# Folding expert biases into the expert weights, and one transpose of denominators for both image halves, in an attention and mixture-of-experts kernel

## Chip, cores and metric

The kernel runs on one core of one Trainium2 chip. The metric is the device time of one execution in microseconds (us); the time before is the median of three runs. One further execution was recorded by the hardware profiler; its span is 1886.6 us.

A core has five engines with queues of their own: PE (TensorE, matrix products and transposes, with weight loads listed as PEld), DVE (VectorE), ACT (ScalarE), POOL (GpSimd) and SP (SyncE, which here only issues transfers). Each works through its instructions in a fixed order and waits for the others by semaphores.

## The reference, cut to what matters

Four images of 32 x 128 x 128 numbers pass through two layers, all in float32.

```python
# layer 0, per image: 4096 tokens of 128 channels
energy = q^T q / (|q_i| |q_j|);  attn = softmax(energy)
x = gamma * (q attn^T) + q
# layer 1, on the same numbers, read as tokens of 128
t = t + linear_attention(ln(t), Wk, Wq, Wv)      # 8 heads
n = ln(t)                                        # mean 0 over the 128 numbers of a row
p = softmax(n @ router_w + router_b); top 2 of 8 experts, renormalised
t = t + sum over the two chosen e of p_e * (n @ expert_w[e] + expert_b[e])
```

The softmax of layer 0 needs one denominator per token; the kernel keeps the denominators as columns (one number per partition) and has to divide a tile in which tokens lie along the row. The expert bias is weighted with the gate `p_e` of its expert.

## The kernel before

A generator `attend` writes the attention of image b. Another generator, `layer1`, writes layer 1 of image b-1; its steps are dealt out between the steps of `attend`, so that both run beside each other. Layer 1 of the last image has nothing to run beside: it forms the tail (`alone`).

The attention step, and the transfers that turn a tile of exponentials for its second use:

```python
pe = ps_e.tile(...); nc.tensor.matmul(pe[:, c0:], qn[jc][:, ts(j, P)], qn[i][:, c0:], ...)   # L276
nc.scalar.activation(pr[:, c0:], pe[:, c0:], AF.Exp, accum_out=sums[:, t, i : i + 1])        # L278
nc.tensor.matmul(po[:, lo:hi], qT[...], w, ...)                                              # L244
nc.vector.transpose(Fb[:, :, :, j, :], pr)                                                   # L285
for a in range(4):
    for q in range(4):
        nc.sync.dma_start(G[ts(q, S), a]..., F[ts(a, S), q]...)                              # L299
# 56 units later: nc.tensor.matmul(pg, qT, G) L213, row sums of G on ACT L218, o += pg on DVE L223
```

The division (one call for each of four quarters of an image; `s` is the half of the channels' rows):

```python
rd = reciprocal(den); rd = rd * gam
def divide(kc):
    df = work.tile([P, 8, HW2, 2], F32, tag="wide", ...)
    for s in range(2):
        ch = 2 * kc + s
        pb = psum_s(...)
        for j in range(NJ):                                   # NJ = 4
            nc.tensor.transpose(pb[:, ts(j, P)], rd[:, blk : blk + 1].to_broadcast([P, P]), ident)   # L383
        for r2 in range(2):
            rows = slice(r2 * 64, r2 * 64 + 64)
            nc.vector.tensor_tensor(df[s*64 : s*64+64, :, :, r2], o[rows]..., pb[rows]..., ALU.mult) # L387
        if s == 1:
            nc.gpsimd.tensor_tensor(tk, tk, df..., ALU.add)   # L395, T += df
        yield
```

Then row statistics, normalisation, the linear attention (`gram`, `pgv`, `pm`, `pat`), row statistics again (rsf, nbf), the router (`route(0)` for rows of groups 0 to 3, `route(1)` for 4 to 7), and the experts:

```python
gate = stat.tile([P, KT + 12, E], ...)
def transpose_gate(g):
    nc.tensor.transpose(pt[:, :P], gate[:, 4 * g : 4 * g + 16, :]..., ident)      # L563
    gates[g] = work.tile([P, P], ..., tag="gT"); nc.vector.tensor_copy(gates[g], pt[:, :P])   # L565
transpose_gate(0)
yield
for g in range(KT // 4):                                      # 8 groups of 4 blocks of 128 rows
    nc.tensor.matmul(pb, gates[g], ebd..., start=True, stop=True)                 # L571, bias of 4 blocks
    nc.vector.tensor_tensor(acc, T[:, ts(g, 4), :], pb..., ALU.add)               # L573
    yield
    for jj in range(2):
        for jk in range(2):
            nc.tensor.matmul(py, xn[:, k, :], ew_sb[:, 0:4, :], ...)              # L581
            for e in range(4): acc[j] = py[e] * gate[k, e] + acc[j]               # DVE, L583
            yield
            nc.tensor.matmul(py, xn[:, k, :], ew_sb[:, 4:8, :], ...)              # L588
            for e in range(4): tmp[jk, e] = py[e] * gate[k, 4 + e]                # ACT, L590
            yield
        # POOL: three adds, L594, L595, L599 (fold tmp, add it to acc)
        if jj == 0 and g + 1 < KT // 4:
            transpose_gate(g + 1)
    # four output transfers from acc, L603
```

Of the kernel before, what the change touches and what calls it, by code (L numbers as in the profile page):

```python
# [10 lines left out]
F32 = mybir.dt.float32  # L11
BF16 = mybir.dt.bfloat16
AF = mybir.ActivationFunctionType
ALU = mybir.AluOpType
# [5 lines left out]
def kernel(  # L20
# [35 lines left out]
    nc = tc.nc  # L56
    P = 128
# [42 lines left out]
    rw_sb = const.tile([P, E], F32, tag="rw", name="rw_sb")  # L100
    rb_sb = const.tile([P, 1, E], F32, tag="rb", name="rb_sb")
    ew_sb = const.tile([P, E, D], F32, tag="ew", name="ew_sb")
    ebd = const.tile([P, 4, D], F32, tag="eb", name="ebd")
    nc.vector.memset(ebd, 0.0)
    at_sb = const.tile([P, NH, D], F32, tag="at", name="at_sb")
    wvx = const.tile([P, NH, D + E], F32, tag="wvx", name="wvx")
    matx = const.tile([P, D + 2 * E], F32, tag="matx", name="matx")
# [5 lines left out]
    def load_weights():  # L113
        nc.scalar.dma_start(gam, gamma.partition_broadcast(P))
        nc.scalar.dma_start(rb_sb[:, 0, :], router_b.partition_broadcast(P))
        nc.scalar.dma_start(rw_sb, router_w)
        for j in range(4):
            nc.scalar.dma_start(ebd[E * j : E * j + E, j, :], expert_b)
        nc.scalar.dma_start(ew_sb, expert_w.rearrange("e d c -> d e c"))

    def setup_weights():
        raw = big1.tile([P, 3, NH, D], F32, tag="xn", name="raw_w")
        wk_sb, wq_sb, wv_sb = raw[:KQ, 0], raw[:KQ, 1], raw[:, 2]
        nc.scalar.dma_start(wk_sb, wk.rearrange("h k d -> k h d"))
        nc.scalar.dma_start(wq_sb, wq.rearrange("h k d -> k h d"))
        nc.scalar.dma_start(wv_sb, wv.rearrange("h e d -> e h d"))
        yield
        for g in range(NH // 4):
            pa = psum_t(f"pa_{g}")
            pv = psum_t(f"pv_{g}")  # L130
            for j in range(4):
                h = 4 * g + j
                nc.tensor.matmul(pa[:, ts(j, D)], wk_sb[:, h, :], wq_sb[:, h, :], start=True, stop=True)
                nc.tensor.transpose(pv[:, ts(j, D)], wv_sb[:, h, :], ident)
            nc.vector.tensor_copy(at_sb[:, 4 * g : 4 * g + 4, :], pa.rearrange("p (h d) -> p h d", d=D))
            nc.vector.tensor_copy(wvx[:, 4 * g : 4 * g + 4, :D], pv.rearrange("p (h d) -> p h d", d=D))
            yield
        pw = psum_t("pw")
        for h in range(NH):
            nc.tensor.matmul(pw[:, ts(h, E)], wv_sb[:, h, :], rw_sb, start=True, stop=True)  # L140
        ones = work.tile([P, P], F32, tag="gT", name="ones")
        nc.vector.memset(ones, 1.0)
        nc.tensor.matmul(pw[:, ts(NH, E)], ones, rw_sb, start=True, stop=True)
        nc.vector.tensor_copy(wvx[:, :, D:], pw[:, : NH * E].rearrange("p (h e) -> p h e", e=E))
        nc.vector.tensor_copy(srw[:, 0, :], pw[:, ts(NH, E)])
        nc.vector.tensor_copy(matx[:, D + E :], rw_sb)
        yield

    def tokens(ap, b):
        return ap[b].rearrange("c (s k r) w -> s r c k w", s=2, r=2)  # L150
# [166 lines left out]
    def layer1(b, st, alone):  # L317
# [24 lines left out]
        nc.vector.tensor_reduce(den, st["sums"], AX.X, ALU.add)  # L342
        rd = stat.tile([P, NB], F32, tag="rd", name=f"rd_{b}")
        nc.vector.reciprocal(rd, den)
        nc.vector.tensor_scalar(rd, rd, gam, None, ALU.mult)
        yield

        rsa, nba, sda = (stat.tile([P, KT, 1], F32, tag=nm, name=f"{nm}_{b}", bufs=1) for nm in ("rsa", "nba", "sda"))
        rsf, nbf = (stat.tile([P, KT, 1], F32, tag=nm, name=f"{nm}_{b}", bufs=1) for nm in ("rsf", "nbf"))

        def row_stats(nm, u, rs_all, nb_all):

# [22 lines left out]

        def divide(kc):
            df = work.tile([P, 8, HW2, 2], F32, tag="wide", name=f"df_{b}_{kc}")
            for s in range(2):
                ch = 2 * kc + s
                pb = psum_s(f"pbd_{b}_{ch}")  # L380
                for j in range(NJ):
                    blk = NJ * ch + j
                    nc.tensor.transpose(pb[:, ts(j, P)], rd[:, blk : blk + 1].to_broadcast([P, P]), ident)  # L383
                o = st["o"][ch]
                for r2 in range(2):
                    rows = slice(r2 * 64, r2 * 64 + 64)
                    nc.vector.tensor_tensor(  # L387
                        df[s * 64 : s * 64 + 64, :, :, r2],
                        o[rows].rearrange("p (k w) -> p k w", w=HW2),
                        pb[rows].rearrange("p (k w) -> p k w", w=HW2),  # L390
                        ALU.mult,
                    )
                if s == 1:
                    tk = T[:, ts(kc, 8), :]
                    nc.gpsimd.tensor_tensor(tk, tk, df.rearrange("p k w r -> p k (w r)"), ALU.add)  # L395
                yield
# [56 lines left out]


        lg = stat.tile([P, KT, E], F32, tag="lg", name=f"lg_{b}", bufs=1)
        gate = stat.tile([P, KT + 12, E], F32, tag="gate", name=f"gate_{b}", bufs=1)
        nc.gpsimd.memset(gate[:, KT:, :], 0.0)
        normed = {}

        def attention_rows(u):  # L460
# [17 lines left out]
        def norm_rows(g):  # L478
            xg = work.tile([P, 4, D], F32, tag="grp", name=f"xg_{b}_{g}", bufs=3)
            for j in range(4):  # L480
                normalise(xg[:, j, :], 4 * g + j, rsf, nbf)
            normed[g] = xg

        def expert_rows(g):
# [48 lines left out]
        for u in range(6):  # L533
            if 0 <= u - 1 < 4:
                la = yield from attention_rows(u - 1)
            for g in (2 * u, 2 * u + 1):
                if u < 4 and not alone:
                    transpose_rows(g)
                    yield
            if 0 <= u - 1 < 4:  # L540
                yield from row_stats(f"f{b}", u - 1, rsf, nbf)
                yield
                router_rows(u - 1, la)
                yield
            for g in (2 * u - 4, 2 * u - 3):
                if 0 <= g - 1:
                    expert_rows(g - 1)
                    yield
                if 0 <= g:
                    norm_rows(g)  # L550
                    yield
            if u in (2, 4):
                yield from route(u // 2 - 1)
# [2 lines left out]


        dst = tokens(out, b)
        gates = {}

        def transpose_gate(g):
            pt = psum_s(f"ptg_{b}_{g}")
            nc.tensor.transpose(pt[:, :P], gate[:, 4 * g : 4 * g + 16, :].rearrange("p j e -> p (j e)"), ident)  # L563
            gates[g] = work.tile([P, P], F32, tag="gT", name=f"gT_{b}_{g}", bufs=2)
            nc.vector.tensor_copy(gates[g], pt[:, :P])  # L565

        transpose_gate(0)
        yield
        for g in range(KT // 4):
            pb = psum_s(f"pbe_{b}_{g}")  # L570
            nc.tensor.matmul(pb, gates[g], ebd.rearrange("p j c -> p (j c)"), start=True, stop=True)  # L571
            acc = work.tile([P, 4, D], F32, tag="acc", name=f"acc_{b}_{g}", bufs=2)
            nc.vector.tensor_tensor(acc, T[:, ts(g, 4), :], pb.rearrange("p (j c) -> p j c", c=D), ALU.add)  # L573
            yield
            for jj in range(2):
                tmp = work.tile([P, 2, 4, D], F32, tag="wide", name=f"tmp_{b}_{g}_{jj}")
                for jk in range(2):
                    j = 2 * jj + jk
                    k = 4 * g + j
                    py = psum_y(f"py_{b}_{k}_0")  # L580
                    nc.tensor.matmul(py, xn[:, k, :], ew_sb[:, 0:4, :], start=True, stop=True)  # L581
                    for e in range(4):
                        nc.vector.scalar_tensor_tensor(  # L583
                            acc[:, j, :], py[:, ts(e, D)], gate[:, k, e : e + 1], acc[:, j, :], ALU.mult, ALU.add
                        )
                    yield
                    py = psum_y(f"py_{b}_{k}_1")
                    nc.tensor.matmul(py, xn[:, k, :], ew_sb[:, 4:8, :], start=True, stop=True)  # L588
                    for e in range(4):
                        nc.scalar.activation(  # L590
                            tmp[:, jk, e, :], py[:, ts(e, D)], AF.Copy, scale=gate[:, k, 4 + e : 5 + e]
                        )
                    yield
                nc.gpsimd.tensor_tensor(tmp[:, :, 0:2], tmp[:, :, 0:2], tmp[:, :, 2:4], ALU.add)  # L594
                nc.gpsimd.tensor_tensor(tmp[:, :, 0], tmp[:, :, 0], tmp[:, :, 1], ALU.add)  # L595
                if jj == 0 and g + 1 < KT // 4:
                    transpose_gate(g + 1)
                rows = acc[:, 2 * jj : 2 * jj + 2, :]
                nc.gpsimd.tensor_tensor(rows, rows, tmp[:, :, 0], ALU.add)  # L599
            for s in range(2):  # L600
# [15 lines left out]
    for b in range(B):  # L616
# [3 lines left out]
        if b == 0:  # L620
            for kc, begin, end in ((1, 0, 5), (2, 6, 20), (3, 25, 45)):
                streams.append((prep(0, kc, states[0]), begin, end, 10))
            streams.append((setup_weights(), 50, 60, 4))
        else:
            streams.append((layer1(b - 1, states[b - 1], False), 7, 97, 161))
        if b + 1 < B:
# [58 lines left out]
```

## Time and profile before

| what | value | where from |
|---|---|---|
| time | 1888.73 us (1886.93 to 1889.08) | median of three runs |
| PE busy | 1799.0 us, 95% of the span | profile, engines |
| DVE, ACT, POOL busy | 909.5, 974.6, 293.7 us | profile, engines |
| mean granted PE clock | 0.983 | profiled run |
| layer 1 of the last image, alone | from about 1732 us to the end | timeline |
| L571, bias product | 64 instructions (2 for each float32 product) | groups |
| L563, transposes of gates | 32 | groups |
| L383, transposes of denominators | 128 | groups |

Busy time is the union of an engine's instructions in the trace. One float32 product of 128x512 appears as two matmul instructions. Matmuls overlap in the records, so that what one costs is read from the distance between starts in the timeline, not from its duration.

### The profile page before, as it was taken

The page shows a single profiled execution, that of the slowest core. Times are in us where ns is not written, and L with a number is a line of the kernel's source. Part 1 is how long each engine was busy: PE and PEld are TensorE (multiplying, and loading weights), DVE is VectorE, ACT ScalarE, POOL GpSimd, SP SyncE. Part 2 cuts the span into 40 slices and gives each one's busy share as a digit, 9 for nine tenths or more (in the row PEclk, how much of TensorE's full clock was granted, in tenths as well). Part 3 has the DMA queues.
Part 4 walks back from the last instruction along what each step waited for, and adds up shares of the span by engine and source line. Part 5 has one row for each costly group of instructions (what it writes and reads, how often), then busy time and mean ns, then how long its engine had stood idle before and what let it go on. Part 6 is the DMA issues. An engine that isn't in the chain of part 4 may idle for free.

```text
span 1886.6 us, 21105 instructions
## 1 busy us (share of the span) xinstructions
PE 1799.0 (95%) x5474; PEld 915.4 (49%) x5474; DVE 909.5 (48%) x2201; ACT 974.6 (52%) x3117; POOL 293.7 (16%) x279
## 2 busy tenths in 40 slices
PE   6999999998999999999999999999899999999678
PEld 4444544454555444455555444445465544444533
DVE  3343224345364454636355455453536445554576
ACT  3454444446457454555556655454554755554455
POOL 0000000002010122212000022220300012221336
PEclk9999999999999999999999999999999999999789
DMA  5333343332233232342233323234233223335001
GB/s 119 80 84 87 78 104 91 89 89 64 61 95 83 65 89 65 86 105 64 64 85 81 92 62 90 68 88 99 53 79 81 72 63 92 81 74 119 1 11 34
DMA packets 142247, 145.68 MB, mean 77 GB/s; under 512 B 32528, under 2 KB 84784, under 8 KB 142128
## 3 DMA queue, kind: packets, MB, share of 16 engines
q1 hardware_dynamic: 138496, 142.73, 31.5%
q10 hardware_dynamic: 3632, 1.60, 0.4%
q8 instruction: 45, 0.74, 0.2%
q14 instruction: 74, 0.61, 0.1%
HBM read 18.38 MB, written 8.39 MB: 14 GB/s over the span
## 4 chain that ended last, share of the span: by engine, by line
PE 81%; DVE 7%; SPq 4%; POOL 3%; ACT 2%; DMA 1%; issue 1%; ACTq 0%; POOLq 0%; DVEq 0%
PE po L244 23%; PE pe L276 20%; PE pg L213 18%; PE py L588 5%; PE py L581 5%; SPq L299 4%; PE pbe L571 1%; PE pat L468 1%; PE pgram L413 1%; DVE F L285 1%; PE ptd L255 1%; POOL rsa L111 1%; DVE df L387 1%; POOL T L395 1%; PE ptn L199 1%
## 5 line engine op out<-in xcount | busy, mean ns | idle before, releaser
L278 ACT ACTIVATE pr<-pe 128x512 f32<-128x512 f32 (+1 forms) x576 | 322.7, 560 | 519.6 <-PE pe L276 513.9
L244 PE MATMUL po<-pr,qT 128*128 128x512 f32 (+3 forms) x1152 | 551.1, 561 | 16.4 <-ACT pr L278 11.6
L285 DVE STREAM_TRANSPOSE F<-pr 128x512 f32<-128x512 f32 x448 | 311.4, 704 | 354.0 <-ACT pr L278 336.5
L276 PE MATMUL pe<-qn,qn 128*128 128x512 f32 x896 | 459.7, 595 | 0.0
L213 PE MATMUL pg<-G,qT 128*128 128x512 f32 x896 | 440.8, 594 | 1.7 <-DVE o L223 1.6
L244 PEld LDWEIGHTS po<-pr,qT 128*128 128x128 f32 x1152 | 213.3, 191 | 249.0 <-issue 182.9
L218 ACT ACTIVATE junk<-G 128x512 bf16<-128x512 f32 x448 | 277.1, 626 | 3.6 <-DMA G<-F 2.8
L213 PEld LDWEIGHTS pg<-G,qT 128*128 128x128 f32 x896 | 167.4, 191 | 196.0 <-issue 186.8
L590 ACT ACTIVATE tmp<-py,gate 128x128 f32<-128x128 f32 x512 | 146.3, 368 | 172.1 <-PE py L588 171.1
L583 DVE SCALAR_TENSOR_TENSOR acc<-py,gate,acc 128x128 f32<-128x128 f32 x512 | 177.7, 349 | 118.3 <-PE py L581 104.6
L276 PEld LDWEIGHTS pe<-qn,qn 128*128 128x128 f32 x896 | 160.9, 191 | 145.3 <-issue 144.4
L223 DVE TENSOR_TENSOR o<-o,pg 128x512 f32<-128x512 f32 x112 | 76.6, 684 | 184.4 <-PE pg L213 183.7
L594 POOL TENSOR_TENSOR tmp<-tmp 128x512 f32<-128x512 f32 x64 | 81.2, 1269 | 534.6 <-ACT tmp L590 534.6
L581 PE MATMUL py<-ew_sb,xn 128*128 128x512 f32 x256 | 132.7, 601 | 1.9 <-ACT tmp L590 1.2
L588 PE MATMUL py<-ew_sb,xn 128*128 128x512 f32 x256 | 131.9, 597 | 2.2 <-DVE acc L583 1.4
L278 ACT ACTIVATION_READ_ACCUMULATOR pr<-pe 128x1 f32 x576 | 114.5, 199 | 0.0
L111 POOL TENSOR_TENSOR rn<-ss,neg_half 128x8 f32<-128x8 f32 x16 | 26.2, 1639 | 500.4 <-DVE ss L185 500.4
L276 PE MATMUL pe<-qn 128*128 128x512 f32 (+3 forms) x256 | 90.3, 444 | 0.0
L218 ACT ACTIVATION_READ_ACCUMULATOR junk<-G 128x1 f32 x448 | 88.5, 198 | 0.0
L370 ACT ACTIVATE xn<-T,nba,rsa 128x128 f32<-128x128 f32 x128 | 51.9, 481 | 55.1 <-DVE nba L367 55.1
L111 POOL TENSOR_TENSOR rsf<-dm_f,neg_half 128x8 f32<-128x8 f32 x16 | 26.3, 1642 | 342.5 <-DVE dm_f L365 342.5
L588 PEld LDWEIGHTS py<-ew_sb,xn 128*128 128x128 f32 x256 | 48.5, 191 | 61.9 <-issue 53.0
(121 smaller groups left out, 1416.5 us busy)
## 6 DMA issues: line engine op xcount, KB each, us to landing
G<-F SPq DMA_DIRECT2D x1792, 64.0 KB, 2.0
xx<-in_x_dram SPq DMA_DIRECT2D x64, 128.0 KB, 2.8
T<-in_x_dram SPq DMA_DIRECT2D x16, 512.0 KB, 7.1
out_dram<-acc SPq DMA_DIRECT2D x128, 64.0 KB, 1.8
ew_sb<-in_L_ffn_expert_w_dram ACTq DMA_DIRECT2D x1, 512.0 KB, 5.4
raw_w<-in_L_attn_Wv_dram ACTq DMA_DIRECT2D x1, 512.0 KB
raw_w<-in_L_attn_Wk_dram ACTq DMA_DIRECT2D x1, 256.0 KB
raw_w<-in_L_attn_Wq_dram ACTq DMA_DIRECT2D x1, 256.0 KB
```

The source lines that it names most:

```text
L213: nc.tensor.matmul(pg.rearrange("p (a f) -> p a f", a=4), st["qT"][i][:, ib, :], G[:, :, ib], start=(ib == 0), stop=(ib == NJ - 1),)
L218: nc.scalar.activation(junk, G[:, :, ib], AF.Copy, accum_out=st["sums"][:, NJ * i + ib, jc : jc + 1])
L223: nc.vector.tensor_tensor(o, o, pg.rearrange("p (a j c) -> p a j c", a=4, c=S), ALU.add)
L244: nc.tensor.matmul(po[:, lo:hi], qT[blk // NJ][:, blk % NJ, :], w, start=(count[0] == 1), stop=(count[0] == total))
L276: nc.tensor.matmul(pe[:, c0:], qn[jc][:, ts(j, P)], qn[i][:, c0:], start=True, stop=True)
L278: nc.scalar.activation(pr[:, c0:], pe[:, c0:], AF.Exp, accum_out=sums[:, t, i : i + 1])
L285: nc.vector.transpose(Fb[:, :, :, j, :], pr)
L581: nc.tensor.matmul(py, xn[:, k, :], ew_sb[:, 0:4, :], start=True, stop=True)
L583: nc.vector.scalar_tensor_tensor(acc[:, j, :], py[:, ts(e, D)], gate[:, k, e : e + 1], acc[:, j, :], ALU.mult, ALU.add)
L588: nc.tensor.matmul(py, xn[:, k, :], ew_sb[:, 4:8, :], start=True, stop=True)
L590: nc.scalar.activation(tmp[:, jk, e, :], py[:, ts(e, D)], AF.Copy, scale=gate[:, k, 4 + e : 5 + e])
L594: nc.gpsimd.tensor_tensor(tmp[:, :, 0:2], tmp[:, :, 0:2], tmp[:, :, 2:4], ALU.add)
```

## The change

It has two parts.

**Expert biases.** A row `n` out of the layer norm has mean 0 over its 128 entries. If `W' = W + (1/128) (b - colsum(W))`, with the same row added to each row of W, then `(n + 1) @ W' = n @ W + b`: the 1 brings in `colsum(W) + b - colsum(W) = b`, and `n` against a constant column gives 0. So the expert weights are changed once, at set-up (two products with a matrix of ones and four DVE operations), the rows are normalised with a bias that is 1 larger (`nbo`), and the bias product, the transposes of gates, their copies and the separate start of `acc` go away.

**Denominators.** Halves s = 0 and 1 are put side by side into one 128x128 tile for each j (64 columns of each), gamma is applied while it is filled, and one transpose serves both. `divide` has three steps then, not two.

```diff
-    ebd = const.tile([P, 4, D], F32, tag="eb", name="ebd")
-    nc.vector.memset(ebd, 0.0)
...
+        eb = work.tile([P, E, D], F32, tag="wide", name="eb")
+        nc.scalar.dma_start(eb, expert_b.partition_broadcast(P))
+        for h in range(2):
+            half = ew_sb[:, 4 * h : 4 * h + 4, :]
+            pc = psum_t(f"pc_{h}")
+            nc.tensor.matmul(pc, ones, half, start=True, stop=True)
+            pe3 = pc.rearrange("p (e d) -> p e d", d=D)
+            dev = eb[:, 4 * h : 4 * h + 4, :]
+            nc.vector.tensor_tensor(dev, dev, pe3, ALU.subtract)
+            nc.vector.scalar_tensor_tensor(half, dev, 1.0 / D, half, ALU.mult, ALU.add)
+            yield
...
-        nc.vector.tensor_scalar(rd, rd, gam, None, ALU.mult)
...
-            for s in range(2):
-                ch = 2 * kc + s
-                pb = psum_s(f"pbd_{b}_{ch}")
-                for j in range(NJ):
-                    blk = NJ * ch + j
-                    nc.tensor.transpose(pb[:, ts(j, P)], rd[:, blk : blk + 1].to_broadcast([P, P]), ident)
+            pb = psum_s(f"pbd_{b}_{kc}")
+            wide = work.tile([P, NJ, 2, 64], F32, tag="grp", name=f"rdx_{b}_{kc}", bufs=3)
+            for s in range(2):
+                one = rd[:, NJ * (2 * kc + s) : NJ * (2 * kc + s + 1), None]
+                nc.vector.tensor_scalar(wide[:, :, s], one.to_broadcast([P, NJ, 64]), gam, None, ALU.mult)
+            yield
+            for j in range(NJ):
+                nc.tensor.transpose(pb[:, ts(j, P)], wide[:, j].rearrange("p s c -> p (s c)"), ident)
...
-                normalise(xg[:, j, :], 4 * g + j, rsf, nbf)
+                normalise(xg[:, j, :], 4 * g + j, rsf, nbo)
...
                 yield from row_stats(f"f{b}", u - 1, rsf, nbf)
+                nc.vector.tensor_scalar(nbo[:, ts(u - 1, 8)], nbf[:, ts(u - 1, 8)], 1.0, None, ALU.add)
...
-        transpose_gate(0)
-        yield
         for g in range(KT // 4):
-            pb = psum_s(f"pbe_{b}_{g}")
-            nc.tensor.matmul(pb, gates[g], ebd.rearrange("p j c -> p (j c)"), start=True, stop=True)
             acc = work.tile([P, 4, D], F32, tag="acc", name=f"acc_{b}_{g}", bufs=2)
-            nc.vector.tensor_tensor(acc, T[:, ts(g, 4), :], pb.rearrange("p (j c) -> p j c", c=D), ALU.add)
-            yield
...
                         nc.vector.scalar_tensor_tensor(
-                            acc[:, j, :], py[:, ts(e, D)], gate[:, k, e : e + 1], acc[:, j, :], ALU.mult, ALU.add
+                            acc[:, j, :], py[:, ts(e, D)], gate[:, k, e : e + 1],
+                            T[:, k, :] if e == 0 else acc[:, j, :], ALU.mult, ALU.add,
                         )
...
-                if jj == 0 and g + 1 < KT // 4:
-                    transpose_gate(g + 1)
...
-            streams.append((setup_weights(), 50, 60, 4))
+            streams.append((setup_weights(), 50, 62, 6))
```

The number of steps after which `layer1` is dealt out (161 between 7% and 97% of an image's attention) is left as it is.

More of the change, by code (lines that the diff above doesn't have):

```diff
@@ L116, in load_weights @@
         nc.scalar.dma_start(rw_sb, router_w)
-        for j in range(4):
-            nc.scalar.dma_start(ebd[E * j : E * j + E, j, :], expert_b)
         nc.scalar.dma_start(ew_sb, expert_w.rearrange("e d c -> d e c"))
@@ L140, in setup_weights @@
             nc.tensor.matmul(pw[:, ts(h, E)], wv_sb[:, h, :], rw_sb, start=True, stop=True)
-        ones = work.tile([P, P], F32, tag="gT", name="ones")
+        ones = work.tile([P, P], F32, tag="sq", name="ones", bufs=1)
         nc.vector.memset(ones, 1.0)
@@ L344, in layer1 @@
         nc.vector.reciprocal(rd, den)
-        nc.vector.tensor_scalar(rd, rd, gam, None, ALU.mult)
         yield
         rsa, nba, sda = (stat.tile([P, KT, 1], F32, tag=nm, name=f"{nm}_{b}", bufs=1) for nm in ("rsa", "nba", "sda"))
-        rsf, nbf = (stat.tile([P, KT, 1], F32, tag=nm, name=f"{nm}_{b}", bufs=1) for nm in ("rsf", "nbf"))
+        rsf, nbf, nbo = (stat.tile([P, KT, 1], F32, tag=nm, name=f"{nm}_{b}", bufs=1) for nm in ("rsf", "nbf", "nbo"))
         def row_stats(nm, u, rs_all, nb_all):
@@ L377, in divide @@
             df = work.tile([P, 8, HW2, 2], F32, tag="wide", name=f"df_{b}_{kc}")
+            pb = psum_s(f"pbd_{b}_{kc}")
+            wide = work.tile([P, NJ, 2, 64], F32, tag="grp", name=f"rdx_{b}_{kc}", bufs=3)
             for s in range(2):
-                ch = 2 * kc + s
-                pb = psum_s(f"pbd_{b}_{ch}")
-                for j in range(NJ):
-                    blk = NJ * ch + j
-                    nc.tensor.transpose(pb[:, ts(j, P)], rd[:, blk : blk + 1].to_broadcast([P, P]), ident)
-                o = st["o"][ch]
+                one = rd[:, NJ * (2 * kc + s) : NJ * (2 * kc + s + 1), None]
[4 more added lines that the diff above has]
+            for s in range(2):
+                own = slice(s * 64, s * 64 + 64)
+                o = st["o"][2 * kc + s]
                 for r2 in range(2):
@@ L387, in divide @@
                     nc.vector.tensor_tensor(
-                        df[s * 64 : s * 64 + 64, :, :, r2],
+                        df[own, :, :, r2],
                         o[rows].rearrange("p (k w) -> p k w", w=HW2),
-                        pb[rows].rearrange("p (k w) -> p k w", w=HW2),
+                        pb[own].rearrange("p (k w) -> p k w", w=HW2),
                         ALU.mult,
@@ L455, in layer1 @@
         lg = stat.tile([P, KT, E], F32, tag="lg", name=f"lg_{b}", bufs=1)
-        gate = stat.tile([P, KT + 12, E], F32, tag="gate", name=f"gate_{b}", bufs=1)
-        nc.gpsimd.memset(gate[:, KT:, :], 0.0)
+        gate = stat.tile([P, KT, E], F32, tag="gate", name=f"gate_{b}", bufs=1)
         normed = {}
@@ L558, in layer1 @@
         dst = tokens(out, b)
[L559 to L565, printed above, removed]
-        transpose_gate(0)
-        yield
         for g in range(KT // 4):
-            pb = psum_s(f"pbe_{b}_{g}")
-            nc.tensor.matmul(pb, gates[g], ebd.rearrange("p j c -> p (j c)"), start=True, stop=True)
             acc = work.tile([P, 4, D], F32, tag="acc", name=f"acc_{b}_{g}", bufs=2)
-            nc.vector.tensor_tensor(acc, T[:, ts(g, 4), :], pb.rearrange("p (j c) -> p j c", c=D), ALU.add)
-            yield
             for jj in range(2):
```

## Prediction

> **What bounds the kernel now.** I began with the page's engine shares and its chain that ended last.
>
> ```profile
> PE 1799.0 (95%) x5474; PEld 915.4 (49%) x5474; DVE 909.5 (48%) x2201; ACT 974.6 (52%) x3117; POOL 293.7 (16%) x279
> PE 81%; DVE 7%; SPq 4%; POOL 3%; ACT 2%; DMA 1%; issue 1%; ACTq 0%; POOLq 0%; DVEq 0%
> ```
>
> PE looks like the bound. To see whether this holds in every stage, I cut the span into windows (columns: stage, its length, then busy us and instructions of PE, PEld, DVE, ACT and POOL, granted PE clock, DMA share, GB/s).
>
> ```profile
> 560.00:700.00 140.00, 139.93 (x394) 67.46 (x393) 70.97 (x165) 80.73 (x254) 19.95 (x20) 1.00 0.32 78
> 700.00:850.00 150.00, 149.48 (x410) 71.34 (x409) 68.66 (x139) 78.11 (x265) 29.26 (x32) 1.00 0.36 87
> 850.00:1000.00 150.00, 143.15 (x506) 79.84 (x506) 80.91 (x218) 78.13 (x242) 22.68 (x13) 0.97 0.30 72
> 1750.00:1800.00 50.00, 35.62 (x210) 30.61 (x211) 30.97 (x136) 25.22 (x61) 14.80 (x9) 0.81 0.00 1
> 1800.00:1886.00 86.00, 68.87 (x166) 30.48 (x164) 63.27 (x214) 45.82 (x150) 47.01 (x50) 0.90 0.11 25
> ```
>
> While experts run beside attention (560 to 850), PE has no gap: 289.4 of 290 us. Around the division (850 to 1000) it idles 7 us per image. Only the tail from 1732 differs: PE idles there and DVE is nearly as busy.
>
> What a removed instruction costs is the distance of starts. The PE timeline (start, length, instruction):
>
> ```profile
> 1644.17 1.02 PE L213 MATMUL pg<-G,qT 128*128 128x512 f32 x2
> 1645.03 1.02 PE L571 MATMUL pbe<-ebd,gT 128*128 128x512 f32 x2
> 1645.89 1.02 PE L276 MATMUL pe<-qn,qn 128*128 128x512 f32 x2
> ...
> 1319.37 0.60 PE L383 MATMUL pbd<-ident,rd 128*128 128x128 f32 x4
> 1319.81 1.02 PE L276 MATMUL pe<-qn,qn 128*128 128x512 f32 x2
> ```
>
> A bias product takes 1645.89 - 1645.03 = 0.86 us of PE, as does every other 128x512 product; four transposes take 0.44 us, 0.11 each.
>
> **What the Trainium skill says.** "Perfetto Trace Analysis", Identifying the Most-Contended Engine: busy share of matmuls is a poor measure of the distance to the roofline, as matmuls are pipelined. The trace agrees: a pair is listed with 1.02 us and costs 0.86; so I count starts. "TensorE: Matmul & The Clock Gate", Part 4: a 128x128 transpose lasts some 275 ns in a kernel, mostly latency. The trace has a median of 273 ns for L383, yet a cost of 110 ns in a row. "VectorE: DVE Perf Modes", The TRN2 errata: a float32 tensor_tensor takes (N+151)/0.96 ns, 691 ns for N = 512; the trace has 687 ns for L573. I use the formula for the new 256-element fills of `wide`: (256+151)/0.96 = 424 ns, an estimate and rather an upper limit. The first-named TensorE page, Part 1: the clock halves after an idle window of some 3.4 us. The tail shows it: 0.52 granted between 1745 and 1760.
>
> **The change, part by part. Beside attention (images 0 to 2).** Removed from PE: 3 x 8 = 24 bias products x 0.86 = 20.6 us; 24 transposes of gates x 0.11 = 2.6 us; of 128 transposes of denominators half go, 16 per image, 48 x 0.11 = 5.3 us. Sum 28.5 us. The first two lie in stretches without a gap on PE, so I count them in full; the third partly falls into waits, but there a quarter now needs one PSUM tile and one turn of PE, not two, which should ease the same waits.
>
> On DVE 24 x (0.687 + 0.284) = 23 us go (L573, L565), and 24 x 0.42 + 12 x 0.17 (`nbo`, as the 8-column L365) = 12 us come. DVE is half idle there: worth nothing.
>
> Set-up: 2 products x 0.86 = 1.7 us on a PE without gaps; four DVE operations of about 0.7 us. The broadcast of 512 KB of biases is issued in the same step in which DVE needs it; the weights of that size landed in 5.4 us. If DVE really waits for it, tiles of exponentials back up, but there are six of them. I charge 1 us. Net beside attention: -28.5 + 2.7 = -25.8 us.
>
> **The tail.** Each group of four blocks is a strict PE sequence:
>
> ```profile
> 1831.23 1.02 PE L571 MATMUL pbe<-ebd,gT 128*128 128x512 f32 x2
> ...
> 1835.52 0.27 PE L563 MATMUL ptg<-ident,gate 128*128 128x128 f32 x1
> ...
> 1839.07 1.02 PE L571 MATMUL pbe<-ebd,gT 128*128 128x512 f32 x2
> ```
>
> The period is 7.84 us: eight expert products (6.87) + bias (0.86) + transpose (0.11). Without the last two it is 6.87, if DVE keeps up: its four accumulations of a block take 1.51 us, 6.04 a group; ACT needs 4 x 1.14 = 4.6, POOL 2 x (1.27 + 0.73 + 0.73) = 5.5. PE stays the bound. Eight groups x 0.97 = 7.8 us.
>
> There is a second gain. Between the first gates and the steady run PE waits:
>
> ```profile
> 1804.43 0.28 DVE L530 TENSOR_TENSOR gate<-oh,dn 128x128 f32<-128x128 f32 x1
> ...
> 1815.79 0.68 DVE L573 TENSOR_TENSOR acc<-T,pbe 128x512 f32<-128x512 f32 x1
> 1816.59 0.34 DVE L583 SCALAR_TENSOR_TENSOR acc<-py,gate,acc 128x128 f32<-128x128 f32 x1
> ...
> 1819.87 0.20 PEld L563 LDWEIGHTS ptg<-ident,gate 128*128 128x128 f32 x2 [0.82 <-DVE gate L530]
> ```
>
> The gates of groups 0 to 3 are there at 1804.7, and two blocks of products lie in PSUM since 1801; but the first accumulation comes at 1816.6, because acc begins with the bias, and its gate transpose stands in PE's queue behind transposes that wait for ACT. Moreover, the transpose for group 1 takes in 16 blocks, hence gates of the second half, which are ready only at 1819.8. After the change accumulation can start at 1804.7. DVE is then busy with statistics and routing, with some 3.7 us idle to 1820; with the 0.97 us of bias work gone it can fit about 13 more accumulations, three blocks, before 1820: 3 x 1.72 = 5 us. That rests on the order in which the build lays DVE's instructions, so I take half: 2.5 us. The division in the tail: the extra fills of quarters 0 and 1 lie under the 10.1 us load of T, and later ones lose their second turn of PE (`pbd` at 1763.1, among other transposes); I take 1 us gain. Tail: 7.8 + 2.5 + 1 = 11.3 us.
>
> **Sum.** 1888.7 - 25.8 - 11.3 = 1851.6; I say **1851 us**, a ratio of 0.980, on the very border of 2%.
>
> **Rivals.** (1) *The SP queue becomes the bound.* Sixteen issues for a tile take 10.0 us, and four bare attention steps take 4 x 3 x 0.86 = 10.3 us of PE: near. For it: the chain runs through these issues from 1710 to 1732, and `layer1`, with some six steps fewer while still dealt out as 161, ends at about 93.5% of an image, leaving a longer bare stretch. Against it: 100 to 200 is bare attention with PE busy 100.00 of 100 us, while SP makes 134 issues, 84 us at the 0.63 between issues in a row. It would give back up to 8 us: 1859. (2) *Waits around the division grow.* ACT's eight normalisations in one run block exponentials (PE waits 5 us at 1347 for ACT). The three-step division moves these runs against the diagonal tiles, where PE has nothing else to do; three images x 3 us either way: 1842 to 1860. (3) *DVE bounds the tail.* Its work from 1804.7 on is 66 us less 7.5; it could end at 1863, against 1879 now. If the build starts accumulation at once, the tail gains 15 us, not 11: 1847. (4) *The removed bias work was hidden anyway*, as PE's records are modelled. Then only the set-up cost would be seen: 1891. Windows without a gap and the exact 0.86 spacing speak against it.
>
> **Range and chances.** The counted PE work (36 us with the tail's groups) is firm; the reordering of waits I put at 8 us either way beside attention (three divisions at about 3 us each) and 5 us in the tail (from no gain beyond the count to DVE's limit). As these need not fall together, I take about 12 us on each side: 1839 to 1864. The border of 2% is 1851.0, so faster by over 2% and within 2% are even: 0.49 and 0.50. A loss of over 2% would need a new 38 us wait: 0.01.
>
> **What would show it right or wrong.** L571, L563, L565 and L573 gone, L383 at 64, PE busy near 1764; the stages with experts still without a PE gap but shorter by 8 to 9 us per image; the tail's group period 6.87 us; the first L583 of the tail soon after the first `gate`. It is wrong if PE gaps open where there were none (then ask what they wait for: G's transfers mean rival 1, ACT rival 2), or if the tail's period stays above 7 us with DVE full.

## The result, and the profile after

The changed kernel takes 1865.45 us (median of 4 runs, 1860.99 to 1865.79) against 1888.9 us before: a ratio of 0.9872, with a 95% interval of 0.9855 to 0.9889. The gain is 23.5 us; 37.1 had been worked out, and the time lies 1.5 us above the range.

The page of the changed kernel, engine shares and the chain that ended last:

```profile
PE 1765.7 (95%) x5318; PEld 890.3 (48%) x5318; DVE 893.4 (48%) x2184; ACT 972.8 (52%) x3117; POOL 293.5 (16%) x275
PE 78%; DVE 12%; POOL 4%; ACT 2%; SPq 2%; DMA 1%; issue 1%; DVEq 0%; POOLq 0%; ACTq 0%
```

PE lost 33.3 us of work, but the span only 22.7: PE's gaps grew from 87.6 to 98.2 us. The chain runs less through PE (78%, not 81%) and more through DVE (12%, not 7%). Stages of the changed kernel (length, then busy us and instructions of PE, PEld, DVE, ACT and POOL, granted PE clock, DMA share, GB/s):

```profile
560.00:700.00 140.00, 139.85 (x414) 69.42 (x413) 67.42 (x175) 83.68 (x265) 18.54 (x18) 1.00 0.33 81
700.00:850.00 150.00, 149.71 (x404) 71.05 (x403) 70.39 (x141) 78.69 (x268) 32.20 (x34) 1.00 0.37 88
850.00:1000.00 150.00, 141.67 (x493) 77.24 (x492) 81.74 (x223) 77.24 (x240) 22.75 (x13) 0.98 0.30 71
```

Beside the experts PE still has no gap (289.56 of 290 us). Around the division it now idles 8.3 us, where it idled 6.9. The timeline of the expert stage and of the tail:

```profile
1622.50 1.02 PE L587 MATMUL py<-ew_sb,xn 128*128 128x512 f32 x2
1623.35 1.02 PE L579 MATMUL py<-ew_sb,xn 128*128 128x512 f32 x2
1624.21 1.02 PE L285 MATMUL pe<-qn,qn 128*128 128x512 f32 x2
...
1794.37 0.28 DVE L541 TENSOR_TENSOR gate<-oh,dn 128x128 f32<-128x128 f32 x1
...
1798.76 0.35 DVE L581 SCALAR_TENSOR_TENSOR acc<-py,gate,T 128x128 f32<-128x128 f32 x1
...
1821.04 1.88 PE L579 MATMUL py<-ew_sb,xn 128*128 128x512 f32 x4
...
1827.90 1.88 PE L579 MATMUL py<-ew_sb,xn 128*128 128x512 f32 x4
```

No bias product stands between the expert products any more; a group of eight in the tail takes 1827.90 - 1821.04 = 6.86 us (7.84 before), and the first accumulation follows the first gates by 4.4 us (12.2 before). The expert half of the change did what was counted. The division did not. What PE waited for (total us, times, longest), first in the kernel before, then in the changed one:

```profile
PE po L244 <- ACT pr L278: 11.6, 11, 1.9
...
PE ptd L255 <- ACT gd L257: 9.0, 3, 5.1
PE pbd L383 <- DVE df L387: 8.9, 3, 7.8
PE pgram L413 <- ACT xn L370: 8.5, 2, 5.4
...
PE pg L213 <- DVE o L223: 1.6, 2, 0.8
```

```profile
PE pgram L425 <- ACT xn L378: 28.8, 6, 19.3
PE po L253 <- ACT pr L287: 17.4, 12, 4.6
...
PE pg L222 <- DVE o L232: 6.3, 6, 1.4
```

The products `po` wait longer for ACT, and `pg` for DVE. The growth of `pgram` is smaller than it looks: 24.8 of its 28.8 us lie in the tail, where the kernel before already waits 17.4 us, in front of `pgram` and of the division's `pbd` together. The 9.0 us of `ptd`, the diagonal tiles' transposes, are gone. To see which stage the loss belongs to, I took six starts from each timeline: the first energy product (`pe`) of images 0 and 1, the last one of image 3, the tail's first `T += df`, its first `gate`, and the end. All in us:

| profile of | to first product | image 0 | images 1 to 3 | to first `T += df` | to first `gate` | to the end | span |
|---|---|---|---|---|---|---|---|
| before | 19.7 | 354.7 | 1355.4 | 15.8 | 58.8 | 82.2 | 1886.6 |
| changed | 21.6 | 358.2 | 1334.0 | 17.4 | 63.2 | 69.6 | 1863.9 |
| changed, again | 19.3 | 358.2 | 1334.0 | 17.3 | 63.2 | 69.5 | 1861.6 |
| bias part alone | 19.2 | 358.2 | 1330.6 | 17.6 | 59.1 | 69.6 | 1854.3 |
| division alone | 19.3 | 354.6 | 1364.9 | 14.7 | 63.0 | 80.8 | 1897.3 |

Both kernels with the new division are the slower ones of their pair in images 1 to 3, and need 4 us more up to the first gate. (The profile of the division alone is of a run of 1899.07 us, 4.1 under the median of its runs.)

### The profile page after: what moved, and what is told of

It is laid out like the page before. It is cut to its first block, busy times and chain, and to the rows that moved or that the text cites. A ratio compares the mean times of both kernels' runs of the same rounds, so it can differ in the third digit from the quotient of the medians.

```text
span 1863.9 us, 20794 instructions
## 1 busy us (share of the span) xinstructions
PE 1765.7 (95%) x5318; PEld 890.3 (48%) x5318; DVE 893.4 (48%) x2184; ACT 972.8 (52%) x3117; POOL 293.5 (16%) x275
## 4 chain that ended last, share of the span: by engine, by line
PE 78%; DVE 12%; POOL 4%; ACT 2%; SPq 2%; DMA 1%; issue 1%; DVEq 0%; POOLq 0%; ACTq 0%
PE po L253 22%; PE pe L285 20%; PE pg L222 18%; PE py L579 5%; PE py L587 5%; DVE df L399 2%; SPq L308 2%; DVE F L294 2%; POOL rsa L109 1%; PE pat L479 1%; PE ptd L264 1%; POOL T L407 1%; ACT xn L378 1%; POOL rn L109 1%; POOL rsf L109 1%
## 5 line engine op out<-in xcount | busy, mean ns | idle before, releaser
L253 PE MATMUL po<-pr,qT 128*128 128x512 f32 (+3 forms) x1152 | 552.7, 562 | 21.3 <-ACT pr L287 17.4
L581 DVE SCALAR_TENSOR_TENSOR acc<-py,gate,acc 128x128 f32<-128x128 f32 x384 | 132.7, 349 | 11.5
L587 PE MATMUL py<-ew_sb,xn 128*128 128x512 f32 x256 | 130.2, 600 | 1.2 <-ACT tmp L589 1.2
L579 PE MATMUL py<-ew_sb,xn 128*128 128x512 f32 x256 | 129.2, 594 | 2.1 <-DVE acc L581 2.0
L581 DVE SCALAR_TENSOR_TENSOR acc<-py,gate,T 128x128 f32<-128x128 f32 x128 | 44.7, 349 | 114.5 <-PE py L579 109.8
## 6 DMA issues: line engine op xcount, KB each, us to landing
eb<-in_L_ffn_expert_b_dram ACTq DMA_DIRECT2D x1, 512.0 KB, 10.3
```

Of the source, the lines that this page charges most:

```text
L253: nc.tensor.matmul(po[:, lo:hi], qT[blk // NJ][:, blk % NJ, :], w, start=(count[0] == 1), stop=(count[0] == total))
L581: nc.vector.scalar_tensor_tensor(acc[:, j, :], py[:, ts(e, D)], gate[:, k, e : e + 1], T[:, k, :] if e == 0 else acc[:, j, :], ALU.mult, A ...
```

## The experiments

**The two parts apart.** First the bias part with the old division, then the new division with the old biases.

```diff
 # e1_bias_only: changed kernel, divide() of before
+        nc.vector.tensor_scalar(rd, rd, gam, None, ALU.mult)
-            wide = work.tile([P, NJ, 2, 64], ...)   # fills, yield, 4 transposes
+            for s in range(2): ... 4 transposes of rd columns each, two steps
 # e2_div_only: kernel before, divide() of the change
```

> The bias part alone; the division is the old one (gamma in rd, two PSUM tiles and eight transposes a quarter). Theory A, the new division costs more than it saves: beside attention 24 bias products and gate transposes fewer, 23.2 us, less 2.8 us of set-up; 2.7 us lost before the first product, as in the changed kernel; from the first gate to the end of the tail 12.7 us less, as in the changed kernel; tail up to the first gate as in the kernel before. Sum 30 us less than before: 1859 us, 6 us faster than the full change. Rival B, the division brought its 6 us and the bias part is short of its sum: 1871 us, slower than the full change.

Measured: 1855.99 us (1851.29 to 1856.12), ratio 0.9819 [0.9805, 0.9832]: -32.7 us.

> The new division alone, biases as before. Theory A: tail 4 us longer up to the first gate (two fills held for 2.3 us each while GpSimd adds to T), one fill held for 1.9 us in each image beside attention and PE gaps around it; 5 us of PE work less. 1889 to 1894 us, no faster than before. Rival B: 64 transposes fewer and one PSUM turn a quarter: 1883 us.

Measured: 1903.18 us (1898.86 to 1903.67), ratio 1.0069 [1.0056, 1.0081]: +14.5 us. So the bias part brings more than the whole change, and the division, meant to save, costs. The two do not add: -32.7 + 14.5 = -18.2, where the change as a whole gives -23.5 (-26.2 when repeated, below). The division costs more beside the old biases than on top of the bias part; why was not taken apart. The waits of PE with the division alone:

```profile
PE pgram L416 <- ACT xn L369: 27.6, 4, 18.3
PE po L244 <- ACT pr L278: 14.3, 11, 4.6
...
PE pg L213 <- DVE o L223: 6.0, 6, 1.3
```

These three are close to those of the changed kernel, without any of its bias part. What follows looks for the reason in the division.

**Was the first profile typical?** The changed kernel unaltered, and once more with the four small bias loads kept ahead of the expert weights in ACT's queue, as the kernel before has them.

```diff
 # e3_keep_loads
+    ebd = const.tile([P, 4, D], F32, tag="eb", name="ebd"); nc.vector.memset(ebd, 0.0)
+        for j in range(4):
+            nc.scalar.dma_start(ebd[E * j : E * j + E, j, :], expert_b)
 # e5_after_again: no edit
```

> The full change, but the four small loads of the expert biases stay in ScalarE's queue ahead of the expert weights, into a tile that nothing reads. Theory A, the start is later because the weights' loads (2.5 MB with the broadcast biases) are now issued 2.8 us sooner and share the transfers with the first image rows: first product of qn at 19.7 us again instead of 21.6, time 1863 us, 2 to 2.7 us less than the full change. Rival B, the late start is chance or comes from elsewhere: 1865.5 us and 21.6 us.

> The full change once more, unaltered, as the measure for the others on this chip and for the start. If the late first product (21.6 us in its first trace) is a property of the load order, it stands at 21.6 again and the time is 1865.5 us. If it was one slow transfer of that execution, as the bias part alone and the early fills suggest (same load order, 19.2 us), the product starts at 19.2 to 19.6 us and the median is 1862 to 1864 us.

Measured: 1861.43 us (1859.61 to 1862.78) with the loads, 1862.52 (1857.18 to 1864.73) without. The 1.1 us lie within the spread, so the order of loads is not shown to matter. The late first product (21.6 us) belongs to that one execution: in the other profiles here of kernels with this order of loads it starts at 18.9 to 20.0 us.

**The fills.** In the changed kernel the fill of `wide` stands directly behind a `T += df` on GpSimd. The timeline of image 1 and of the tail:

```profile
427.28 2.35 POOL L407 TENSOR_TENSOR T<-T,df 128x1024 f32<-128x1024 f32 x1 [12.15 <-DMA G<-F]
427.87 2.18 DVE L390 TENSOR_SCALAR rdx<-rd,gam 128x256 f32<-128x256 f32 x2
...
435.83 2.34 POOL L407 TENSOR_TENSOR T<-T,df 128x1024 f32<-128x1024 f32 x1 [6.20 <-DVE df L399]
435.87 2.33 DVE L370 TENSOR_TENSOR dm_a<-bs_a 128x8 f32<-128x8 f32 x1
...
440.77 1.65 ACT L378 ACTIVATE xn<-T,nba,rsa 128x128 f32<-128x128 f32 x4 [6.34 <-DVE nba L375]
...
443.04 2.07 PE L253 MATMUL po<-pr,qT 128*128 128x512 f32 x2 [4.63 <-ACT pr L287]
...
1731.21 4.68 POOL L407 TENSOR_TENSOR T<-T,df 128x1024 f32<-128x1024 f32 x2 [34.90 <-DMA T<-in_x_dram]
1731.36 4.68 DVE L390 TENSOR_SCALAR rdx<-rd,gam 128x256 f32<-128x256 f32 x2
```

Two fills take 2.18 us at 427.87 and 4.68 us at 1731.36, and each pair ends within 0.5 us of GpSimd's addition. Five of the 32 fills are held so; the others take 0.35 us. At 435.87 an 8-element subtraction takes 2.33 us, like the addition beside it. Behind it the normalisations come late, and PE waits 4.63 us for ACT. Of the next two kernels one moves the fills, all of an image at once, ahead of any addition; the other moves the addition to VectorE:

```diff
 # e4_early_fill: fills in two instructions behind reciprocal(rd, den), into rows of xn not yet used; those in divide go
+        rdx = xn[:, KT // 2 :, :].rearrange("p (k j) (s c) -> p k j s c", k=4, s=2)
+        for s in range(2):
+            one = rd.rearrange("p (k s j) -> p k s j", s=2, j=NJ)[:, :, s, :, None]
+            nc.vector.tensor_scalar(rdx[:, :, :, s], one.to_broadcast([P, 4, NJ, 64]), gam, None, ALU.mult)
 # e7_add_dve: changed kernel, fills where they were
-                    nc.gpsimd.tensor_tensor(tk, tk, df..., ALU.add)
+                    nc.vector.tensor_tensor(tk, tk, df..., ALU.add)
```

> The full change, but all fills of an image are made at once in two VectorE instructions when the denominators are there, before GpSimd's first addition to T (into rows of xn that are not yet in use). Theory A, a fill that meets an addition of GpSimd is held until its end: no fill over 1.2 us, the third addition of the tail 7.5 us after the first again (9.9 in the full change), tail 4 us shorter, gaps of PE beside attention down by up to 3 us in image 0: 1857 to 1861 us. Rival B, the loss comes from the three-step division as such (its place against the diagonal tiles), not from held fills: gaps beside attention as in the full change, tail alone shorter by 2 us or less: 1863 to 1866 us.

Measured: 1854.71 us (1851.99 to 1855.52), ratio 0.9818 [0.9804, 0.9831]: 7.8 us less than the repeated changed kernel (1862.52). The size fits theory A, the places do not: the third addition of the tail follows the first by 7.5 us as expected, but the tail up to the first gate is only 1.8 us shorter (61.4 against 63.2), and 6.4 us come from images 1 to 3. PE's wait of 4.63 us stays (4.36), and so does the subtraction of 2.33 us ahead of it: no held fill stands behind that wait.

> The full change, but the additions of the division to T on VectorE, not GpSimd; fills stay where the change put them. Theory A, a VectorE instruction that reads two operands from SBUF or runs the fill is held while GpSimd adds: now no fill and no dm_a or sv_a over 1.2 us in the division, tail up to gram 3 to 6 us shorter, time 1855 to 1860 us, although VectorE gets 16 additions of about 1.2 us. Rival B, the fill is slow of itself when its neighbours are dense, or VectorE's load counts: fills of 1.9 to 2.4 us remain, or the time stays at 1864 us or more.

Measured: 1847.0 us (1846.66 to 1847.95), ratio 0.9779 [0.9764, 0.9793]. The fills (duration in ns, min/median/max), first in the changed kernel:

```profile
L390 DVE TENSOR_SCALAR rdx<-rd,gam x32: 338/348/2425, 403.1 to 1733.6; 128x256 f32<-128x256 f32 x32
```

and with the addition on VectorE:

```profile
L390 DVE TENSOR_SCALAR rdx<-rd,gam x32: 311/348/355, 400.1 to 1716.5; 128x256 f32<-128x256 f32 x32
```

Same fill, same place: it is the addition on GpSimd that held it. The subtraction takes 0.16 us now, and PE's wait for ACT behind it falls from 4.63 to 2.53 us. The time is 8 us under the forecast of theory A.

**Is that cost the change's own?** The same edit in the bias part alone and in the kernel before:

```diff
 # e11_bias_add_dve: e1_bias_only;  f1_before_add_dve: kernel before
-                    nc.gpsimd.tensor_tensor(tk, tk, df..., ALU.add)
+                    nc.vector.tensor_tensor(tk, tk, df..., ALU.add)
```

> The bias part, the old division, additions to T on VectorE. Asks what the shared transpose is worth once no fill is held. Predicted for it at first: 16 transposes of 0.11 us an image less on PE, 5.3 us beside attention and 1 us in the tail. If that holds, this run stands 5 to 7 us above the run with the three remedies: 1847 us. If the transposes were hidden in gaps of PE: the same time, 1841 to 1843 us.

Measured: 1839.31 us (1838.87 to 1839.97), ratio 0.9736 [0.9722, 0.9749]: 16.7 us under the bias part, and lower than either forecast. The run with the three remedies (1832.7, below) lies a further 6.6 us lower, within the 5 to 7 us expected.

> The kernel before, with one word altered: T += df of each quarter runs on VectorE, not on GpSimd. With the bias part in place and the old division the same edit gave 16.7 us (1856.0 to 1839.3). Theory A, the GpSimd add is a cost of its own (it takes 2.35 us on a path, and holds VectorE instructions) and was so before the change: about 1872 us, ratio 0.991. Theory B, it became costly only as the biases' removal freed PE and DVE around it: 1885 to 1889.

Measured: 1870.92 us (1870.59 to 1872.04), ratio 0.9892 [0.9877, 0.9907], against 1890.28 us of before beside it: 19.4 us. Theory A holds: the addition on GpSimd had cost no less before the change. The change put new instructions in its way, but GpSimd is not its whole loss: with additions on VectorE the new division still costs 1847.0 - 1839.3 = 7.7 us.

**The third step.** A quarter has three steps, not two; beside attention, work of attention is put in between two steps. Without the third:

```diff
 # e6_two_steps: e4_early_fill;  e12_two_add_dve_late: e7_add_dve, fills kept where they were
-            yield
             for j in range(NJ):
                 nc.tensor.transpose(pb[:, ts(j, P)], wide[:, j]..., ident)
```

> The early fills, and a division of two steps a quarter, as in the kernel before (the step that held the fill is left out). If the remaining gaps beside attention (12.5 us in image 0 with early fills, 10.7 with the old division) come from the place of the statistics against the diagonal tiles, they change: image 0 back to 10 to 11 us of gaps, 1851 to 1853 us. If the place does not matter: 1854 to 1855 us and gaps as with early fills.

Measured: 1847.36 us (1846.74 to 1848.53), ratio 0.9781 [0.9766, 0.9795]: 7.3 us under e4_early_fill, where at most 4 were forecast.

> The full change with additions to T on VectorE and two steps a quarter, but the fills where the change put them, one pair ahead of each quarter. If a fill costs only by being held, nothing is left of that here: the same as with early fills, within 1 us. If a fill in front of the products costs by its own 0.7 us a quarter: 2 to 3 us more.

Measured: 1834.52 us (1833.72 to 1835.08), ratio 0.971 [0.9696, 0.9723]: 12.5 us under e7_add_dve, and 1.8 over the run with early fills (1832.7, below), so a fill in front of the products costs a little even when nothing holds it. The step costs. Its place or its split? Two kernels restore the count of steps without parting fill and transposes:

```diff
 # f2_four_steps_ahead: e12_two_add_dve_late
+        for _ in range(4):
+            yield
         for kc in range(6):
 # f3_empty_step_after: e12_two_add_dve_late
                 yield from divide(kc)
+                yield
```

> The changed kernel with two steps a quarter and adds on VectorE (1834.5 us), and four empty steps ahead of the first quarter: all later work of layer 1 is as late as with three steps a quarter (1847.0 us), but a quarter's fill, transposes and products stay together. Theory A, the third step costs by where it puts statistics and normalisation against the diagonal tiles of attention: 1843 to 1849, here too. Theory B, it costs because it splits the quarter, so that its parts and the steps after it lie further apart: 1834 to 1838.

> The changed kernel with two steps a quarter and adds on VectorE (1834.5 us), and an empty step after each quarter: three steps again, as in the change (1847.0 us), but nothing comes between the fill and its transposes. If the pace of the quarters is what costs (theory A and also the wider reading of B): 1843 to 1849. If the gap between fill and transposes costs: 1834 to 1838.

Measured: 1846.12 us (1844.98 to 1847.43) and 1843.46 us (1842.6 to 1844.45), with the kernel before 1.0 us slower beside them than beside e12_two_add_dve_late. Four empty steps ahead of the division cost 11.6 us, nearly the 12.5 of the third steps; an empty step behind each quarter costs 8.9. So what costs is that layer 1's work comes later within the image's attention, not that a quarter is split. In the profiles, images 1 to 3 take 16.0 us longer with the four steps ahead (1320.8 against 1304.8), and the border to the tail gives 5.0 back (18.1 against 23.1). The stretch of image 3 from the first energy product of row 3 to that of row 5 (columns as in the stages above), first with two steps:

```profile
1304.20:1413.90 109.70, 108.44 (x395) 60.35 (x394) 59.82 (x178) 65.72 (x199) 12.54 (x7) 1.00 0.30 74
```

then with four empty steps ahead:

```profile
1313.20:1428.80 115.60, 109.57 (x400) 60.66 (x399) 65.84 (x196) 65.93 (x199) 11.54 (x7) 1.00 0.30 73
```

and the waits of PE there (total us, times, longest):

```profile
PE po L253 <- ACT pr L287: 2.6, 3, 1.4
PE pg L222 <- DVE o L232: 1.4, 1, 1.4
PE pgram L424 <- ACT xn L378: 1.2, 1, 1.2
PE ptd L264 <- DVE df L398: 0.8, 1, 0.8
```

PE idles 115.60 - 109.57 = 6.0 us in place of 1.3, in six small waits for ACT and DVE; DVE has 6.0 us more to do in this stretch, as part of the quarters has moved into it too. Which wait starts the others was not taken apart. That `pgram` waits for normalisations and that the diagonal tiles' transposes (`ptd`) are among them fits rival 2 of the prediction, but the normalisations and the diagonal as the cause are only argued: the quarters come later as well.

**A better kernel.** All three together (early fills, two steps, addition on VectorE), and the tail's T loaded in quarters, once on e4_early_fill and once on the three:

```diff
 # e8_split_load: e4_early_fill;  e10_plus_split: e9_early_two_add_dve
-        load_tokens(T, b, 0, KT)
+        if alone:
+            for kc in range(4):
+                load_tokens(T[:, ts(kc, 8), :], b, 8 * kc, 8)
```

> The early fills, and in the tail T is loaded in four parts by quarter, the first first. The first addition waits 8.3 us after the denominators, of which VectorE's products take about 5; the load lands 12 us after its issue. If the load is what it waits for, the first addition comes 2.5 to 3 us sooner and the time is 1851 to 1852 us. If the products set it, or SP's sixteen issues delay the last parts, the time stays at 1854 to 1855 us.

> All three remedies on the full change: fills at once, two steps a quarter, additions to T on VectorE. If each removes a wait of its own, the gains add in part: early fills and two steps gave 1847.4, additions on VectorE 1847.0 against 1862.5; 1840 to 1843 us. If they remove the same waits: 1845 to 1847 us.

> As the run with the three remedies, and T of the tail loaded by quarters. With early fills alone the split gave about 1.5 us, within the spread of the runs. Expected 1 to 2 us less than without the split if VectorE's own queue does not set the first addition; otherwise the same.

Measured: e8_split_load 1853.18 us (1851.83 to 1854.11), 1.5 us under e4_early_fill, which their spreads do not separate. e9_early_two_add_dve 1832.7 us (1832.34 to 1833.28), ratio 0.9701 [0.9687, 0.9714]; e10_plus_split 1832.42 us (1831.71 to 1833.26), 0.9699 [0.9685, 0.9712]. Both beat both kernels. The three remedies together end 7 us under the better of the two forecasts; the split load, with 0.3 us where 1 to 2 were expected, brings nothing that the runs separate. With the three, the stage around the division has lost its gaps:

```profile
850.00:1000.00 150.00, 149.02 (x543) 83.40 (x544) 84.82 (x245) 83.25 (x259) 14.23 (x8) 1.00 0.32 78
```

and the chain at the border to the tail runs through issues and the load of T again (start, length, step of the chain), as it did in the kernel before from 1709.8 us on:

```profile
1687.56 0.59 SPq L308
1688.19 0.59 SPq L308
1689.45 0.60 SPq L166
1690.09 8.77 DMA T<-in_x_dram
1699.53 0.68 DVE df L399
```

The images take 1304.1 us, 29.9 less than in the changed kernel, but from the last energy product to the first `T += df` 21.0 us pass, not 17.4: SP's issues for G and T are behind by now and give back 3.6 us.

## Why the prediction failed, point by point

**The counted PE work: right.** L571, L563, L565 and L573 are gone, 64 transposes are left, PE is busy 1765.7 us (some 1764 predicted).

**Bias part beside attention: right.** Predicted -20.6 - 2.6 = -23.2; the bias part alone has -24.8 in images 1 to 3.

**Set-up: right.** Predicted +2.7; image 0 takes 3.5 us more.

**Tail from the first gate on: right, a little low.** Predicted -7.8 - 2.5 = -10.3; the bias part alone has 82.2 - 69.6 = -12.6. The 0.98 us of a group came as counted; the earlier accumulation brought about 4.8, not the half of 5 that I took. Rival 3, DVE as the tail's bound, did not come: the groups still keep PE's 6.86 us.

**The division: wrong.** This is the step that failed: it was counted as -6.3 us and measured +6.5 on top of the bias part (1862.5 against 1856.0). Two sentences carry it: that "there a quarter now needs one PSUM tile and one turn of PE, not two, which should ease the same waits", for -5.3 us, and that the extra fills "lie under the 10.1 us load of T", for -1 us. The runs split this step into three terms, in two series of kernels:

| | additions on GpSimd | additions on VectorE |
|---|---|---|
| fills moved ahead | -7.8 (again to e4) | -1.8 (e12 to e9) |
| third step left out | -7.3 (e4 to e6) | -12.5 (e7 to e12) |
| what the shared transposes then bring, against the bias part | -8.6 (e1 to e6) | -6.6 (e11 to e9) |

The kernel before, measured beside these kernels, has medians of 1888.7 to 1889.3 us, so less than a microsecond means nothing here. The shared transposes, with one PSUM tile in place of two, are worth at least the 6.3 us that I counted, but not where I counted them: between e11 and e9 images 1 to 3 gain 9.4 us, and the way from the last energy product to the first gate grows by 2.6 (78.3 to 80.9). The two things I had put at nothing or near it, where the fills stand and how many steps a quarter takes, cost 15.1 and 14.3 us together. I had costed the fills by DVE's spare time; what counts is when they end. In the tail the fills fell not under the load of T but under the first additions. The way to the first gate grew there by 4.4 us, where I had it shrink by 1; the fills account for 1.8 of it (e4), the rest stays open.

**Rival 2 came true in part.** It named the third step, which does cost by where it puts later work (f2), and ACT's normalisations as the reason, which is not shown; the held fills it did not name. Its size, 3 us "either way" for an image, was fair: the division alone costs 2.9, 3.1 and 3.5 us in images 1, 2 and 3, but on top of the bias part 3.9, 0.7 and -1.3. My sum had left this term out; only the range took it in. **Rival 1** (SP's queue) slept in the changed kernel (17.4 against 15.8 us at the border) and woke in the fastest (21.0). **Rival 4** is out: with the bias part alone images 1 to 3 are 24.8 us shorter, so the removed products had not been hidden.

The repeated profile of the changed kernel gives the balance: the images lie 7.1 us above the working, the division in the tail 5.4, the border 1.5, the set-up 0.8, the rest of the tail 2.4 below. That is 12.4 us, and the late first product of the first profile adds 2.3.

## What to carry to other kernels

When an edit adds small VectorE instructions or a scheduling step, ask what runs on GpSimd at that moment and what the step pushes later, not only whether the engine has time to spare. Count removed PE work by the distance of starts where PE has no gap, as that held to within 2 us here; where PE waits, measure the part by itself before adding it to a sum. After a gain, look at the next queue in line: here the issues of transfers took 3.6 of 29.9 us back.

## What the runs showed of the hardware

A VectorE instruction that starts while GpSimd adds two SBUF tiles can be held to the end of that addition: fills of 0.35 us took up to 2.43, a subtraction of 8 elements 2.33. The Trainium skill has this ("SBUF — State Buffer", Who interferes with whom): the two engines share a port pair as an exclusive lock, which `tensor_scalar` takes in its 2-port mode and `tensor_tensor` with two SBUF inputs on the reading side; the second to come waits for the whole instruction. The trace agrees that both kinds are held, and I should have drawn on it in the prediction. That the fill runs in that mode is not shown, but fits its pace: the early fill of 1024 columns takes 0.75 us, VectorE's addition of as many 1.2. Others were not held: in the profiles of before and after, 44 BATCH_NORM_STATS2 and 9 STREAM_TRANSPOSE, with one operand, and 6 products with one operand in PSUM start inside such an addition and take at most 0.30, 0.71 and 0.69 us, as they do elsewhere. I had not expected the size: the addition of 128x1024 takes 2.35 us on GpSimd and 1.2 on VectorE, and moving 16 of them gained 15.5, 16.7 and 19.4 us in three kernels, though VectorE has more to do then. How much of that is the shorter addition and how much the instructions held was not taken apart.
